# A third Winograd level in five more pairs of a tuned f32 matrix product, and two early sums moved into another round

## The chip, the cores and the metric

The kernel runs on one core of one Trainium2 chip, as one launch. The metric is the device time of that core in microseconds, the median of several runs. The engines are called PE (TensorE, matrix products), DVE (VectorE), ACT (ScalarE), POOL (GpSimd) and SP (SyncE, which here only issues transfers).

## The reference, cut to what matters

Everything is float32. `x` has 32 samples of 128 channels by 2048.

```python
# first half: mix the channels, then a 2048 x 2048 layer with a low-rank update
att = softmax(mlp(cond_128))                       # 32 x 8
agg_w = einsum('bk,koi->boi', att, weight)         # one 128 x 128 kernel per sample
h = einsum('boi,bih->boh', agg_w, x) + agg_b
out = einsum('bsd,od->bso', h, W) + bias           # 4096 x 2048 by 2048 x 2048
upd = einsum('ebsr,eor,e->bso', einsum('bsd,erd->ebsr', h, A), Bf, coeffs * scales)
x = x + out + upd
# second half: grouped convolution, then a small two-layer network on each of 16 heads of permuted columns
c = conv1d(x, conv_weight, groups=4, pad=4) + ctx + bias
t = c[:, perm] as heads of 128
x = x + (gelu(t @ up[h]) @ down[h])[unperm]
```

The low-rank update is folded into the weight: the kernel first makes W' = W plus the sum of the scaled products of A and Bf, and then multiplies the 4096 rows of x by W'. The channel mix acts on the channels of a sample and the layer on the columns, so the mix is applied after the product.

## The kernel before, in words

**The big product.** x W' is made by Winograd's form of Strassen's method: 7 products of half-size blocks stand in the place of 8. The outer level gives seven rounds, in the order `ROUNDS = ("P1", "P2", "P6", "P7", "P5", "P3", "P4")`. Each round works through 8 groups g (512 rows of x each). Inside a round `multiply` (L341) makes a group's 512x1024 by 1024x1024 block with 7 products of the second level; each product is 4 matmuls of 128x128 by 128x512, and the profile counts two passes of PE for every f32 matmul. Results go to a PSUM bank and from there are added by DVE (or copied first by ACT) into accumulators of 128x2048.

**The third level.** In some pairs of groups (g even and g + 1, the table `PAIRS`) two of the seven products, P2 and P4, are not made for each group alone: `multiply_third` (L536) makes them for both groups together with seven products of quarter blocks ("quarters", matmuls of 256 columns, L607). Their weights come from `third_weights` (`P_q`), their inputs from `third_inputs` (`sq`). In the pairs of `MORE` a second family, P3 and P7, is made in that way too (`multiply_more`, L482, quarters at L514, weights `P_v` from `more_weights`, inputs `sv` from `more_inputs`). A group is then left with 5 or 3 products of its own, and a pair has 7 or 14 quarters.

**Between the products.** After each product the function calls `between(j)`, in which the main loop gives other engines something to do: `mixed_kernel` (DVE, 8 chained operations on 128x128 for one k range of a sample's mixing kernel, `ags`), weights' differences for the third level, row sums of W', and the loads of later steps.

**Buffers and queues.** Nearly all tiles of 128x2048 (x, weights, their combinations, accumulators) come from one pool of `SLOTS = 26` buffers through `slot`. The pool gives a new tile the buffer of a tile that was released earlier, and the first write to it waits for the last reader. Every engine works through its instructions in program order, which is written out by hand. SP issues loads of x (`x_load`), of weights and of partial results (`part_load`) and the stores of accumulators. POOL makes `x_combine` (four operations of 128x512, `s_P`), inner weights (16), outer weights and `outer_sums`, and issues some stores itself.

**Early sums.** Rounds P6 and P5 multiply sums of blocks of x, which `outer_sums(g, ts)` makes: eight operations on POOL, and a store of each result (`s1` for P5, `s2` for P6 and P3). For the first `EARLY = 2` groups this is done ahead of P6, and the three x tiles are loaded for it alone:

```python
k_early = g if r == "P2" else -1
if 0 <= k_early < EARLY:
    early_x = [x_load(k_early, *k) for k in ((1, 0), (1, 1), (0, 0))]
def between(j):
    if j == 3 and 0 <= k_early < EARLY:
        outer_sums(k_early, early_x)
```

**The rest.** P1 starts while W' is still being made, block by block (`w_make_two`, stored to DRAM as `wb_d`). Beside the last round and after it come the convolution, the mix (L842, L853) and the per-head networks (L986, L997), which the change does not touch.

Of the kernel before, what the change touches and what calls it, by code (L numbers as in the profile page):

```python
# [17 lines left out]
B = 32  # L18
L = 2048
QW = 512  # L20
KEXP = 8
# [27 lines left out]


PAIRS = {
    "P1": (1, 2, 3), "P2": (0, 1, 2, 3), "P6": (0, 1, 2, 3), "P7": (0, 1, 2, 3),
    "P5": (0, 1, 2, 3), "P3": (0, 1, 2, 3), "P4": (0,),
}
MORE = {"P7": (1, 2), "P3": (1, 2)}
ENDS = ("P1", "P4")
EARLY = 2

# [2 lines left out]
def adaln_ffn_kernel(  # L61
# [355 lines left out]
    def in_pair(r, g):  # L417
        return g // 2 in PAIRS[r]

    rest = []  # L420

    def third_inputs(i, eng):

        (x11, x12), (x21, x22) = (
            [xa[n][:, 1, :, h * NQ : (h + 1) * NQ] for h in range(2)] for n in (i, i + 1)
        )
        tt = eng.tensor_tensor
        t = slot(f"sq_{i}", (P, 4, 2, NQ))
        tt(t[:, 0], x21, x22, ALU.add)
        tt(t[:, 1], t[:, 0], x11, ALU.subtract)  # L430
        rest.append((t[:, 2], x11, x21))
        rest.append((t[:, 3], x12, t[:, 1]))
        if eng is nc.gpsimd:
            sums_rest(eng)
        return {
            "P1": x11, "P2": x12, "P3": t[:, 3], "P4": x22,
            "P5": t[:, 0], "P6": t[:, 1], "P7": t[:, 2],
        }

    def sums_rest(eng):  # L440
        while rest:
            eng.tensor_tensor(*rest.pop(0), ALU.subtract)

    def more_weights(name, rhs):

# [36 lines left out]
    def multiply_more(r, g, lhs, rhs, accs, between, families):  # L482

        px, py = bank(), bank()
        if g % 2 == 0:
            both = [accs]
            held.extend((both, {}, {}))
        both, *sums = held
        if g % 2:
            both.append(accs)  # L490

        def add(ps, *to):
            for si, oi in to:
                for acc in accs:
                    nc.vector.tensor_tensor(acc[:, si, oi], ps, acc[:, si, oi], ALU.add)  # L495

        def product(k, ps, first, last):
            for kc in range(4):
                nc.tensor.matmul(  # L499
                    ps, lhsT=lhs[k][:, bass.ts(kc, P)], rhs=rhs[k][kc],  # L500
                    start=first and kc == 0, stop=last and kc == 3, skip_group_check=True,
                )

        def quarter(n, k):

            quarters, x = families[n]
            qs = sums[n]
            if k in ("P1", "P5", "P2"):
                qs[k] = bank()
            ps = qs[{"P6": "P1", "P7": "P1", "P4": "P1", "P3": "P5"}.get(k, k)]  # L510
            first, last = k in ("P1", "P2", "P5"), k in ("P2", "P3", "P4")
            for i, out in enumerate(halves(ps)):
                for kc in range(2):
                    nc.tensor.matmul(  # L514
                        out, lhsT=x[k][:, 1 - i if n else i, bass.ts(kc, P)],
                        rhs=quarters[i][k][kc],
                        start=first and i == 0 and kc == 0, stop=last and i == 1 and kc == 1,
                        skip_group_check=True,
                    )
            b, h = {  # L520
                "P1": (0, 0), "P2": (0, 0), "P6": (0, 1), "P5": (1, 1), "P7": (1, 1),
                "P3": (0, 1), "P4": (1, 0),
            }[k]
            cols = slice(h * NQ, (h + 1) * NQ)
            for acc in both[b]:
                part = acc[:, :, n, cols]
                nc.vector.tensor_tensor(  # L527
                    part, ps.rearrange("p (s n) -> p s n", s=2), part, ALU.add
                )
                if n:  # L530
                    part = acc[:, 1, 0, cols]
                    nc.vector.tensor_tensor(part, ps[:, NQ : 2 * NQ], part, ALU.add)
            if last:
                done(ps)

        def quarters_of(*nks):  # L536
            if g % 2:
                for n, k in nks:
                    quarter(n, k)

        product("P1", px, True, False)
        add(px, (0, 0))
        between(0)
        quarters_of((0, "P6"), (0, "P5"))
        product("P5", py, True, True)
        add(py, (1, 1), (0, 1))
        done(py)
        between(1)
        quarters_of((1, "P6"), (0, "P7"))
        product("P6", px, False, True)  # L550
        add(px, (0, 1), (1, 1), (1, 0))
        done(px)
        between(2)
        if g % 2 == 0:
            quarter(0, "P1")
            quarter(0, "P2")
            between(3)
            quarter(1, "P1")
            between(4)
            quarter(1, "P2")  # L560
            between(5)
            return
        quarters_of((1, "P5"), (0, "P3"))
        between(3)
        quarters_of((1, "P7"), (0, "P4"))
        between(4)
        quarters_of((1, "P3"))
        between(5)
        quarters_of((1, "P4"))
        held.clear()  # L570
        for b, accs in enumerate(both):
            for (_, new), acc in zip(ADDED[r], accs):
                part_store(new, g - 1 + b, acc, nc.sync)
# [648 lines left out]
    for i, (r, g) in enumerate(steps):  # L1222
        ri = i // NG
        last_round = ri + 1 == len(ROUNDS)
        if i + 1 < len(steps):
            if i + 1 not in xs:
                xs[i + 1] = x_loads(*steps[i + 1])
            if not last_round:
                lhs[i + 1] = x_combine(*steps[i + 1], xs.pop(i + 1))
                if g == 2 * PAIRS[r][0]:  # L1230
                    quarters, quarter_ops = third_weights(r, rhs)
                if in_pair(r, g) and g % 2 == 0 and g > 0 and r != "P6":
                    sq = third_inputs(i, nc.gpsimd)
                    if in_more(r, g):
                        sv = more_inputs(i)
                if r in MORE and g == 2 * MORE[r][0] - 1:
                    more, more_ops = more_weights(r, rhs)
        if i == 0:
# [41 lines left out]
        if last_round:  # L1280
            stage(k0, stage_first)

        k_early = g if r == "P2" else -1
        if 0 <= k_early < EARLY:
            early_x = [x_load(k_early, *k) for k in ((1, 0), (1, 1), (0, 0))]

        def between(j):

            if j == 3 and 0 <= k_early < EARLY:
                outer_sums(k_early, early_x)  # L1290

            b = (ri - 1) * (NG - 2) + g + 1 if ri > 0 else g - (NG - 2)
            if (g in range(1, NG - 1) if ri > 0 else g >= NG - 2) and b < B:
                k = j - 2 if r == "P5" and g == 1 else j
                if 0 <= k < KEXP // 2:
                    mixed_kernel(b, (2 * k, 2 * k + 1))
            if ri == 0 and j == 2:
                for k in blocks[6 + 2 * g : 8 + 2 * g]:
                    wt[k] = w_load(*k)
            if j < 4 and quarter_ops:  # L1300
                nc.vector.tensor_tensor(*quarter_ops.pop(0), ALU.subtract)
            if j < 4 and more_ops:
                nc.vector.tensor_tensor(*more_ops.pop(0), ALU.subtract)
            if i == NG - 1 and j == 3:
                olds_load(i + 1)
            if j == 3 and ahead and steps[i + 2][0] == "P6":
                xs[i + 2] = x_loads(*steps[i + 2])
            if ri == 0 and j in (1, 3) and unsummed:
                row_sums(*unsummed.pop())
            if ri == 0 and j == 5 and unsummed_first:  # L1310
                t = unsummed_first.pop(0)
                tt = nc.vector.tensor_tensor
                tt(wsum[:, 0, 0], wsum[:, 0, 0], t[:, 0, 0], ALU.add)
                tt(wsum[:, 0], wsum[:, 0], t[:, 1], ALU.add)
            if last_round:
                if j == 1 and i + 1 < len(steps):
                    lhs[i + 1] = x_combine(*steps[i + 1], xs.pop(i + 1))
                    olds_load(i + 1)
                if j == 4 and i + 2 < len(steps):
                    xs[i + 2] = x_loads(*steps[i + 2])  # L1320
                if j in (2, 4):
                    stage(k0 + j // 2, stage_first)
                if j % 2:
                    stage_third(k0 + j // 2)
                else:
                    stage(k0 + j // 2, stage_second)
# [10 lines left out]
            multiply(r, g, lhs.pop(i), rhs, olds.pop(i), between)  # L1337
        xa.pop(i - 1, None)
        ss.pop(i - 1, None)
        if in_pair(r, g) and g % 2 == 0 and (g == 0 or r == "P6" or last_round):  # L1340
            sq = third_inputs(i, nc.gpsimd if r in ENDS else nc.vector)
        next(chain, None)
        if i > 4:
# [95 lines left out]
```

## Time and profile before

| | |
|---|---|
| median of 3 runs | 2577.21 us (2575.98 to 2579.15) |
| profiled execution | 2577.27 us, span 2575.5 us, granted clock 0.999 |
| largest group of PE | L986 and L997, 460 us each (the last third of the span) |
| DVE, largest group | L714, `ags`, 195.5 us in 224 records |
| POOL, largest group | L735, 174.5 us |
| P1 starts / P2 / P6 (first matmul on PE) | 45.9 us / 296.4 / 482.8 |
| P7 / P5 / P3 / P4 | 669.4 / 853.1 / 1038.8 / 1222.6 |

The profiled execution lies within 0.1 us of the median, so its rows stand for the median run. A row of a timeline gives the start, the duration, the engine, the line, the operation with its tiles, the shape and the number of records; in brackets stands the idle time of the engine before it and what ended it. Buffer and group numbers are left out of names there.

### The profile page before, as it was taken

To read this page: it belongs to the slowest core of one execution; us is meant where nothing else is said; L and a number is where in the kernel's file an instruction comes from. 1 tells how busy PE (TensorE), PEld (TensorE's weight loads), DVE (VectorE), ACT (ScalarE), POOL (GpSimd) and SP (SyncE) were. 2 spreads that over 40 slices of the span, in tenths; PEclk is the share of its full clock that TensorE was granted. 3 is DMA by queue.
4 is the path that set the end of the run, shared out by engine and by line. 5 is a ranking of instruction groups with operands and counts; after the bars stand their busy time and mean duration, and the time that the engine had idled before them with its cause. 6 is when DMAs were issued, how large, how long until landed. Compare 5 with 4: busy or idle time off the path is not lost.

```text
span 2575.5 us, 22121 instructions
## 1 busy us (share of the span) xinstructions
PE 2564.0 (100%) x7142; PEld 1355.4 (53%) x7142; DVE 1579.5 (61%) x2450; ACT 532.3 (21%) x1099; POOL 1394.2 (54%) x1158
## 2 busy tenths in 40 slices
PE   9999999999999999999999999999999999999999
PEld 4455555555566555566554554455555554455543
DVE  5665576666585576675476666666666666667611
ACT  0000000000000000000011244444444444444432
POOL 7431788878997736989432134444344434434222
PEclk9999999999999999999999999999999999999999
DMA  7452588579366486574866887787777877777432
GB/s 322 182 211 113 198 338 344 212 285 370 151 249 263 196 337 273 221 287 168 281 230 210 279 290 266 224 259 230 226 223 234 252 246 223 222 251 237 164 123 90
DMA packets 186867, 610.42 MB, mean 237 GB/s; under 512 B 17664, under 2 KB 91904, under 8 KB 142336
## 3 DMA queue, kind: packets, MB, share of 16 engines
q1 hardware_dynamic: 147936, 473.48, 51.2%
q0 software_dynamic: 32992, 132.14, 15.2%
q10 hardware_dynamic: 5824, 3.40, 0.5%
q8 instruction: 57, 0.93, 0.1%
q14 instruction: 58, 0.48, 0.1%
HBM read 372.45 MB, written 202.94 MB: 223 GB/s over the span
## 4 chain that ended last, share of the span: by engine, by line
PE 95%; DVE 3%; DMA 2%; issue 0%; SPq 0%; POOLq 0%; ACT 0%; ACTq 0%; DVEq 0%
PE bank L594 26%; PE bank L986 17%; PE bank L997 17%; PE bank L607 9%; PE bank L357 7%; PE bank L842 6%; PE bank L750 4%; PE bank L499 3%; PE bank L223 3%; PE bank L514 2%; DMA w<-in_WT 1%; DVE ags L714 1%; DMA xt<-in_xT 0%; DVE u L527 0%; DVE u L495 0%
## 5 line engine op out<-in xcount | busy, mean ns | idle before, releaser
L986 PE MATMUL bank<-t,ws 128*128 128x512 f32 x1024 | 460.3, 592 | 0.0
L997 PE MATMUL bank<-gl,ws 128*128 128x512 f32 x1024 | 460.1, 592 | 0.0
L1004 POOL DMA_INDIRECT out<-t,orow x128 | 152.3, 1189 | 535.8 <-DVE t L1002 452.5
L989 ACT ACTIVATE gl<-bank 128x512 f32<-128x512 f32 x512 | 306.1, 598 | 433.3 <-PE bank L986 414.1
L997 PEld LDWEIGHTS bank<-gl,ws 128*128 128x128 f32 x1024 | 194.6, 190 | 232.9 <-issue 231.5
L986 PEld LDWEIGHTS bank<-t,ws 128*128 128x128 f32 x1024 | 194.6, 190 | 226.6 <-issue 222.2
L594 PE MATMUL bank<-P_t,s_P 128*128 128x512 f32 x640 | 284.3, 592 | 0.4 <-ACT m_P L589 0.4
L1002 DVE TENSOR_TENSOR t<-bank,t 128x512 f32<-128x512 f32 x128 | 88.4, 690 | 320.2 <-PE bank L997 309.4
L735 POOL TENSOR_TENSOR x<-x,fb 128x512 f32<-128x512 f32 x128 | 174.5, 1392 | 198.9 <-DMA x<-in_x 136.4
L741 ACT ACTIVATE bank<-w,aggb 128x512 f32<-128x512 f32 x128 | 80.8, 684 | 880.3 <-DMA w<-w_d 867.8
L283 POOL TENSOR_TENSOR xt<-xt,xt 128x512 f32<-128x512 f32 x120 | 159.0, 1358 | 104.6 <-DMA xt<-in_xT 88.4
L714 DVE SCALAR_TENSOR_TENSOR ags<-mix,att_bc,ags 128x128 f32<-128x128 f32 x224 | 195.5, 873 | 4.7
L594 PEld LDWEIGHTS bank<-P_t,s_P 128*128 128x128 f32 x640 | 121.4, 190 | 140.4 <-issue 136.6
L587 DVE TENSOR_TENSOR u<-bank,u 128x512 f32<-128x512 f32 x156 | 101.6, 686 | 147.4 <-PE bank L594 135.1
L594 PE MATMUL bank<-wo_P,s_P 128*128 128x512 f32 x416 | 184.7, 592 | 0.0
L319 POOL TENSOR_TENSOR s_P<-xt 128x512 f32<-128x512 f32 x52 | 68.8, 1323 | 204.0 <-DMA xt<-in_xT 164.2
L970 POOL DMA_INDIRECT t<-hx_d,row x128 | 131.1, 1025 | 56.6 <-issue 25.6
L587 DVE TENSOR_TENSOR p<-bank,p 128x512 f32<-128x512 f32 x96 | 64.6, 687 | 117.8 <-PE bank L594 117.1
L594 PEld LDWEIGHTS bank<-wo_P,s_P 128*128 128x128 f32 x416 | 79.0, 190 | 89.2 <-issue 87.3
L842 PE MATMUL bank<-va,tw_l 128*128 128x256 f32 x512 | 121.5, 380 | 0.7 <-DVE va L826 0.7
L853 ACT ACTIVATE cv<-bank,ctxb 128x128 f32<-128x128 f32 x256 | 73.0, 368 | 234.6 <-PE bank L842 234.6
L753 DVE TENSOR_TENSOR x<-bank,x 128x512 f32<-128x512 f32 x128 | 88.1, 690 | 50.8 <-POOL x L735 21.9
(242 smaller groups left out, 3869.0 us busy)
## 6 DMA issues: line engine op xcount, KB each, us to landing
xt<-in_xT SPq DMA_DIRECT2D x84, 1024.0 KB
u<-u_d SPq DMA_DIRECT2D x40, 1024.0 KB
wo_P<-wb_d SPq DMA_DIRECT2D x36, 1024.0 KB
u<-c_d SPq DMA_DIRECT2D x64, 512.0 KB
x<-in_x SPq DMA_DIRECT2D x32, 1024.0 KB
xg<-x SPq DMA_DIRECT2D x256, 128.0 KB
hx_d<-x1t SPq DMA_DIRECT2D x32, 1024.0 KB
hx_d<-ht SPq DMA_DIRECT2D x32, 1024.0 KB
```

The lines of the kernel that those rows point to most:

```text
L283: nc.gpsimd.tensor_tensor(out[:, i, j], a[:, i, j], b[:, i, j], op)
L357: nc.tensor.matmul(ps, lhsT=lhs[k][:, bass.ts(kc, P)], rhs=rhs[k][kc], start=first and kc == 0, stop=last and kc == 3, skip_group_check=True,)
L587: nc.vector.tensor_tensor(to, ps, to, ALU.add)
L594: nc.tensor.matmul(ps, lhsT=lhs[k][:, bass.ts(kc, P)], rhs=rhs[k][kc], start=first and kc == 0, stop=last and kc == 3, skip_group_check=True,)
L607: nc.tensor.matmul(out, lhsT=sq[k][:, i, bass.ts(kc, P)], rhs=quarters[i][k][kc], start=first and i == 0 and kc == 0, stop=last and i == 1 ...
L714: nc.vector.scalar_tensor_tensor(ag, mix[:, k], att, ag, ALU.mult, ALU.add)
L735: nc.gpsimd.tensor_tensor(xt[:, f], xt[:, f], late["fb"][:, f], ALU.add)
L842: nc.tensor.matmul(out, lhsT=w[:, 2 * i + r], rhs=rhs, start=first and r == 0, stop=last and r == 1, skip_group_check=True,)
L986: nc.tensor.matmul(pu, lhsT=w[:, m * P : (m + 1) * P], rhs=t[:, 0], start=True, stop=True)
L989: nc.scalar.activation(gl[m], pu, AF.Gelu)
L997: nc.tensor.matmul(pd, lhsT=w[:, (MC + m) * P : (MC + m + 1) * P], rhs=gl[m], start=(m == 0), stop=(m == MC - 1),)
L1004: nc.gpsimd.indirect_dma_start(out=out, out_offset=bass.IndirectOffsetOnAxis(ap=orow[:, g, h : h + 1], axis=0), in_=t[:, 1], in_offset=None,)
```

## The change

Five pairs get one level more: P1's pair 0, until now made by `multiply`, is made by `multiply_third`; pair 1 of P2, pair 1 of P6, pair 3 of P7 and pair 3 of P3 get the second family. The inputs of the third level are made in parts (`sums_rest(eng, n)`), so that some of the operations can follow later. In the rounds of `MORE` the 48 calls of `mixed_kernel` are handed out from a list, one after each of the first four products in groups 2 and 4 and two in the other groups from 1 on, where until now the groups 1 to 6 had eight each. `k_early` becomes `g - 6` in P1: the first sums, with their six loads of x and their stores, are issued in P1's groups 6 and 7 and no longer in P2's groups 0 and 1. Row sums of W' are given other places in P1.

```diff
--- before.py
+++ after.py
@@ -49,10 +49,10 @@
 
 
 PAIRS = {
-    "P1": (1, 2, 3), "P2": (0, 1, 2, 3), "P6": (0, 1, 2, 3), "P7": (0, 1, 2, 3),
+    "P1": (0, 1, 2, 3), "P2": (0, 1, 2, 3), "P6": (0, 1, 2, 3), "P7": (0, 1, 2, 3),
     "P5": (0, 1, 2, 3), "P3": (0, 1, 2, 3), "P4": (0,),
 }
-MORE = {"P7": (1, 2), "P3": (1, 2)}
+MORE = {"P6": (1,), "P7": (1, 2, 3), "P3": (1, 2, 3), "P2": (1,)}
 ENDS = ("P1", "P4")
 EARLY = 2
 
@@ -419,17 +419,19 @@
 
     rest = []
 
-    def third_inputs(i, eng):
+    def third_inputs(i, eng, later=False):
 
         (x11, x12), (x21, x22) = (
             [xa[n][:, 1, :, h * NQ : (h + 1) * NQ] for h in range(2)] for n in (i, i + 1)
         )
         tt = eng.tensor_tensor
         t = slot(f"sq_{i}", (P, 4, 2, NQ))
-        tt(t[:, 0], x21, x22, ALU.add)
-        tt(t[:, 1], t[:, 0], x11, ALU.subtract)
-        rest.append((t[:, 2], x11, x21))
-        rest.append((t[:, 3], x12, t[:, 1]))
+        rest.append((t[:, 0], x21, x22, ALU.add))
+        rest.append((t[:, 1], t[:, 0], x11, ALU.subtract))
+        if not later:
+            sums_rest(eng, 2)
+        rest.append((t[:, 2], x11, x21, ALU.subtract))
+        rest.append((t[:, 3], x12, t[:, 1], ALU.subtract))
         if eng is nc.gpsimd:
             sums_rest(eng)
         return {
@@ -437,9 +439,9 @@
             "P5": t[:, 0], "P6": t[:, 1], "P7": t[:, 2],
         }
 
-    def sums_rest(eng):
-        while rest:
-            eng.tensor_tensor(*rest.pop(0), ALU.subtract)
+    def sums_rest(eng, n=4):
+        for _ in range(min(n, len(rest))):
+            eng.tensor_tensor(*rest.pop(0))
 
     def more_weights(name, rhs):
 
@@ -542,6 +544,8 @@
         add(px, (0, 0))
         between(0)
         quarters_of((0, "P6"), (0, "P5"))
+        if g % 2:
+            sums_rest(nc.vector)
         product("P5", py, True, True)
         add(py, (1, 1), (0, 1))
         done(py)
@@ -1222,6 +1226,10 @@
     for i, (r, g) in enumerate(steps):
         ri = i // NG
         last_round = ri + 1 == len(ROUNDS)
+        if g == 0:
+            b = (ri - 1) * (NG - 2) + 2
+            mixes = [(b + n // KEXP, n % KEXP) for n in range((NG - 2) * KEXP)]
+            mixes = [m for m in mixes if m[0] < B]
         if i + 1 < len(steps):
             if i + 1 not in xs:
                 xs[i + 1] = x_loads(*steps[i + 1])
@@ -1229,10 +1237,13 @@
                 lhs[i + 1] = x_combine(*steps[i + 1], xs.pop(i + 1))
                 if g == 2 * PAIRS[r][0]:
                     quarters, quarter_ops = third_weights(r, rhs)
-                if in_pair(r, g) and g % 2 == 0 and g > 0 and r != "P6":
-                    sq = third_inputs(i, nc.gpsimd)
-                    if in_more(r, g):
-                        sv = more_inputs(i)
+                if in_pair(r, g) and g % 2 == 0 and g > 0:
+                    if r != "P6":
+                        sq = third_inputs(i, nc.gpsimd)
+                    elif in_more(r, g):
+                        sq = third_inputs(i, nc.vector, True)
+                if in_more(r, g) and g % 2 == 0:
+                    sv = more_inputs(i)
                 if r in MORE and g == 2 * MORE[r][0] - 1:
                     more, more_ops = more_weights(r, rhs)
         if i == 0:
@@ -1280,7 +1291,7 @@
         if last_round:
             stage(k0, stage_first)
 
-        k_early = g if r == "P2" else -1
+        k_early = g - 6 if r == "P1" else -1
         if 0 <= k_early < EARLY:
             early_x = [x_load(k_early, *k) for k in ((1, 0), (1, 1), (0, 0))]
 
@@ -1290,14 +1301,19 @@
                 outer_sums(k_early, early_x)
 
             b = (ri - 1) * (NG - 2) + g + 1 if ri > 0 else g - (NG - 2)
-            if (g in range(1, NG - 1) if ri > 0 else g >= NG - 2) and b < B:
+            if (g in range(1, NG - 1) if ri > 0 else g >= NG - 2) and b < B and r not in MORE:
                 k = j - 2 if r == "P5" and g == 1 else j
                 if 0 <= k < KEXP // 2:
                     mixed_kernel(b, (2 * k, 2 * k + 1))
+            if r in MORE and 0 < g and j < 4:
+                for _ in range(1 if g in (2, 4) else 2):
+                    if mixes:
+                        b, k = mixes.pop(0)
+                        mixed_kernel(b, (k,))
             if ri == 0 and j == 2:
                 for k in blocks[6 + 2 * g : 8 + 2 * g]:
                     wt[k] = w_load(*k)
-            if j < 4 and quarter_ops:
+            if i and j < 4 and quarter_ops:
                 nc.vector.tensor_tensor(*quarter_ops.pop(0), ALU.subtract)
             if j < 4 and more_ops:
                 nc.vector.tensor_tensor(*more_ops.pop(0), ALU.subtract)
@@ -1305,9 +1321,9 @@
                 olds_load(i + 1)
             if j == 3 and ahead and steps[i + 2][0] == "P6":
                 xs[i + 2] = x_loads(*steps[i + 2])
-            if ri == 0 and j in (1, 3) and unsummed:
+            if ri == 0 and unsummed and (j in (1, 3) and (i, j) != (1, 3) or (i, j) == (3, 2)):
                 row_sums(*unsummed.pop())
-            if ri == 0 and j == 5 and unsummed_first:
+            if (i, j) in ((2, 5), (3, 0), (3, 4), (4, 0)) and unsummed_first:
                 t = unsummed_first.pop(0)
                 tt = nc.vector.tensor_tensor
                 tt(wsum[:, 0, 0], wsum[:, 0, 0], t[:, 0, 0], ALU.add)
@@ -1337,7 +1353,9 @@
             multiply(r, g, lhs.pop(i), rhs, olds.pop(i), between)
         xa.pop(i - 1, None)
         ss.pop(i - 1, None)
-        if in_pair(r, g) and g % 2 == 0 and (g == 0 or r == "P6" or last_round):
+        if in_more(r, g) and r == "P6":
+            sums_rest(nc.vector, 2)
+        elif in_pair(r, g) and g % 2 == 0 and (g == 0 or r == "P6" or last_round):
             sq = third_inputs(i, nc.gpsimd if r in ENDS else nc.vector)
         next(chain, None)
         if i > 4:
```

Lines after L440 are four further down in the changed kernel.

## The prediction

> **What bounds the kernel now.** I read the totals of the page first, then the chain that ended last, then the timelines of PE, POOL and SP around the end of round P1, because that is where the moved sums go.
>
> ```profile
> PE 2564.0 (100%) x7142; PEld 1355.4 (53%) x7142; DVE 1579.5 (61%) x2450; ACT 532.3 (21%) x1099; POOL 1394.2 (54%) x1158
> ...
> PE 95%; DVE 3%; DMA 2%; issue 0%; SPq 0%; POOLq 0%; ACT 0%; ACTq 0%; DVEq 0%
> ```
>
> TensorE works 2564.0 of 2575.5 us. All other engines have idle time, so only two things count: how many passes PE makes, and any new hole in PE. A hole costs its full length. The difference between two kernels that this kernel's measurement can tell from no change is about 0.2%, here 5 us.
>
> PE at the end of P1 (start, duration, operation, number of passes):
>
> ```profile
> 247.61 1.89 PE L607 MATMUL bank<-P_q,xt 128*128 128x256 f32 x8
> 249.34 3.60 PE L594 MATMUL bank<-w,xt 128*128 128x512 f32 x8
> ...
> 267.18 3.60 PE L594 MATMUL bank<-w,xt 128*128 128x512 f32 x8
> 270.62 7.03 PE L594 MATMUL bank<-P_t,s_P 128*128 128x512 f32 x16
> 277.48 7.03 PE L594 MATMUL bank<-w,s_P 128*128 128x512 f32 x16
> ...
> 287.80 5.34 PE L607 MATMUL bank<-P_q,sq 128*128 128x256 f32 x24
> 292.98 1.03 PE L607 MATMUL bank<-w,sq 128*128 128x256 f32 x4
> ...
> 296.44 3.60 PE L594 MATMUL bank<-w,xt 128*128 128x512 f32 x8
> ```
>
> Two prices come from it. A pass of 512 columns takes (284.35 - 277.48)/16 = 0.429 us (284.35 is where the next row starts), a pass of 256 columns (292.98 - 287.80)/24 = 0.216 us. Call E the end of the quarters of group 5, 249.34. Group 7 starts at 267.18, makes P1 (3.43 us) and P5 (3.43 us), and starts its product P6 at 274.05, E + 24.7. From there 10.3 us of group 7 and 12.1 us of quarters remain; P2 starts at 296.44.
>
> POOL over the same time and a little after:
>
> ```profile
> 258.62 1.26 POOL L319 TENSOR_TENSOR s_P<-xt 128x512 f32<-128x512 f32 x1 [36.81 <-DMA xt<-in_xT]
> ...
> 268.70 1.26 POOL L252 TENSOR_TENSOR P_t<-w 128x512 f32<-128x512 f32 x1
> ...
> 289.45 1.27 POOL L319 TENSOR_TENSOR s_P<-xt 128x512 f32<-128x512 f32 x1
> ...
> 327.52 4.93 POOL L283 TENSOR_TENSOR xt<-xt,xt 128x512 f32<-128x512 f32 x4
> 332.75 0.56 POOL L277 DMA_DIRECT2D s_d<-xt  x1 [0.30 <-POOL xt L283]
> ```
>
> The reader sees that POOL cannot begin the end of P1 before x of group 7 lands: it starts 9.3 us after E, and then has 28 operations (combinations of group 7, its third-level inputs, P2's inner weights) until 289.45, 30.8 us. Today the next thing is s_P of P2's group 0. The first sums come only in P2.
>
> **Part 1, third level in five more pairs.** A pair that goes one level deeper, P1's pair 0 from second to third or the others from one family of quarters to two, loses 32 passes of 512 and gains 56 of 256: 56 x 0.216 - 32 x 0.429 = -1.65 us. The five together: -8.25 us, all on PE. Beside it DVE gets 44 evictions of 256 columns and 35 of 2x256, less 2 of 512 (0.41 and 0.69 us each by the timeline of P7's pair 1: 41 us over the whole), and POOL 20 operations of 512 (1.27 to 1.39 us) and 16 of 256 (0.72 to 1.18): 37 to 47 us. I take both as hidden by the 996 and 1181 us in which those engines stand still. Where they are dense the cover can fail: the first pair with two families in P7 and P3 shows stalls of 0.75, 0.64, 0.34 and 1.02 us, 1.4 us a pair, so P2's and P6's new pair could add 0 to 2.8 us. P7's and P3's pair 3 look like P7's pair 2, where PE is busy 45.00 of 45.00 us between 762 and 807, so nothing there. At P1's start POOL now makes third_weights and pair 0's inputs ahead of the weight stores, and later weight loads wait for the buffers of those stores: 0 to 4 us by my walk, 0.5 taken.
>
> **Part 2, mixes spread out.** The same 48 per round, 0.87 us each on average, but 4 fewer in group 2 of P7 and P3, just before those four stalls. They sum to 2.75 us; the gain is 0 to 2.75. I take 1.9, and with the 0.5 above that is -1.4.
>
> **Part 3, the first sums (outer_sums 0 and 1) go from P2's to P1's end.** The removal in P2 gains nothing, PE has no hole over 0.5 us there. The cost is in the addition, and it is one of buffers. The instruction order of the changed kernel with its waits shows that the six extra x tiles take the last free ones of the 26 buffers. The chain, with E' for the end of group 5's quarters in the changed kernel:
> - POOL comes to the sums of group 0 only behind the 28 operations, at E' + 9.3 + 30.8 = 40.1. The eight pieces and two stores cost 4.93 + 0.86 + 4.93 + 0.86 (0.86 is the 0.30 wait and 0.56 issue of the store row): the pieces end at 50.8, the store of s2 is issued by 51.7. In before the second such group took 12.4 us between 343.86 and 356.25, so up to 1.7 more.
> - The load of x for P2's group 0 takes the buffer of xt_000, so it waits for the last piece, 50.8. A 1 MB load landed 7.9 us after its issue at 250.72 in before, with another transfer beside it, and in 5.5 us when alone (issued at 139.86, POOL's start at 145.33). s_P20, 5.0 us, sits on POOL between the two sums and ends at about 63.
> - The load of xt_111, needed by the sums of group 1, takes the buffer of xt_011 and waits until the store of s2 has landed; loads behind it on SP wait too. The stores of these sums landed in 5.5 us at best, 10.6 in the median, 11.9 at worst: 57 to 64, taken as 62 since three more 1 MB transfers run at that time. Then 5.5 to 7.9 us of load: 62.7 to 72, taken as 68.5.
> - The sums of group 1 take 4.93 + 0.86 + 4.93 = 10.7 us: end at 73.4 to 82.7 (up to 1.7 more), taken as 79.
> - ACT's first copy into group 7's accumulator (L593, m_P) has been given the buffer of xt_100, which the last of these pieces reads. The copy, 0.6 us, therefore waits for it. PE's product P6 of group 7 goes into the PSUM bank that this copy empties, so PE stops after P5, at E' + 24.7.
>
> PE resumes at about 79.6 and should have been there at 24.7: a hole of 55 us (74.0 to 85 gives 49.3 to 60). Taken: 54.5, as x may land a little earlier. Behind the waiting copy on ACT are group 7's other copies and the issue of a small store; behind the waiting loads on SP are p1 of P2's group 0 (which takes xt_110's buffer) and the stores of P1's last pair. Nothing of that is late a second time: after the hole PE has 22.4 us of P1 left, and P2's inputs land in those.
>
> One more cost follows from such a hole. The first six passes of the program, 4 of 512 and 2 of 256 columns, would take 2.15 us by the prices above and took 4.36 (1.47 to the next row at 5.83), though the column of the granted clock shows 1.00 there. After a hole of this length I expect the same again, 0 to 2.2 us; taken 2.0.
>
> The Trainium skill ("TensorE: Matmul & The Clock Gate", section "What's actually happening") says that the array drops to half its clock after an idle window of some 3.4 us and needs as long a busy one to come back. An estimate by that page is 3.4 / 2 = 1.7 us for this hole, and the sum would be 0.3 us lower; it speaks against this change, as the holes of before were too short for it.
>
> The Trainium skill ("DMA: Bandwidth & Descriptors", section "Anatomy of one DMA") fits a transfer by 2.0 us plus its bytes over 436 GB/s, which would be 4.4 us for 1 MB by estimate. The landings in this trace are longer, 5.5 at the least; with 4.4 for each the chain would end near 72 and the hole be 47 us, the sum 7.5 us lower; the measured ones decide.
>
> **The sum.** The profiled execution took 2577.27 us (span 2575.5 and 1.8 around it), beside a median of 2577.21, so no conversion is needed. 2577.27 - 8.25 - 1.4 + 54.5 + 2.0 = 2624.1, given as 2624.
>
> **The rivals.**
> - No hole, the other side (faster). If the buffers that the sums give back come in time, only PE's saving is left: 2577.27 - 8.25 - 1.4 = 2567.6, between 2566 and 2571. It decides whether the last piece of the second sums ends before E' + 24.7. For it: POOL is idle for 36.81 us before 258.62, so there is room for 22 us of sums before E. Against it: in POOL's order they stand behind the combination of group 7 and the inner weights, and the first cannot start before x lands. 9%.
> - The hole is only at P2's start. If group 7's copies find a buffer, P2 still needs x and the accumulator p1 of its group 0, and p1's load takes xt_110's buffer, so it waits for the store of s1 and the last piece, 79, and lands in 5.5. P2 would start at E' + 47.1; PE can fill three banks (3 x 3.43 us) before it must wait for one that DVE adds into p1. The hole is then 79 + 5.5 - 47.1 - 10.3 = 27 us: 2577.27 - 8.25 - 1.4 + 27 + 2 = 2596.6. For it: SP's order has that wait as well. Against it: ACT's copy comes first. 5%.
> - DVE or POOL becomes the bound in the deeper pairs on top of the hole: at 1.4 us in each of five pairs, 7 us, 2631. For it: the four stalls in P7 and P3 are DVE's. Against it: pair 2 of P7 without any. 14%, inside the range.
>
> **How the numbers follow.** 72% for the forecast, 14% for it with late engines, 5% for the hole at P2's start alone, 9% for none. The range: the short end of the chain is a hole of 49.3, no slow restart and all of 2.75 gained, 2577.27 - 8.25 + 49.3 - 2.75 = 2615.6; x of group 7 landing in 5.5 in place of 7.9 us takes 2.4 more off, and POOL's 48 operations at the best pitch of the rows (1.22 for 1.26 us) about 2: 2611. The long end is 60 + 2.2 + 2.8 + 4 = 69 us, 2638. 2611 to 2638 leaves out the two rivals with a smaller hole, 14%, and some tail. Faster by over 0.2% is the first rival, 0.09; within 0.2%, 0.01, since no case ends there; slower 0.90.
>
> **What would show it.** PE's timeline of the changed kernel would have one hole of 49 to 60 us after P5 of P1's group 7, released by ACT's copy into m_P, and POOL's timeline the sums of group 1 ending just before. P2 would begin some 52 us later than 296.44, and from there every stage would run at its old length less 1.65 us in each deepened pair. Wrong would be: no hole over 5 us in P1, the sums of both groups ending before group 7's P6, or holes of several us in P2's, P6's, P7's or P3's deeper pairs.

## The result, and the profile after

The changed kernel takes 2624.23 us (median of 6 runs, 2622.44 to 2625.56), beside 2576.60 for the kernel before in the same runs: a ratio of 1.0181, with a 95% interval of 1.0171 to 1.0191. It is 1.8% slower. The profiled execution took 2622.44 us, 45.2 more than the one of before.

The totals of the page after, its row of granted clocks over 40 slices of the span, and the shares of the engines in the chain that ended last:

```profile
PE 2556.7 (98%) x7262; PEld 1378.4 (53%) x7262; DVE 1616.8 (62%) x2527; ACT 533.3 (20%) x1099; POOL 1434.7 (55%) x1194
...
PEclk9999599999999999999999999999999999999999
...
PE 94%; POOL 2%; DMA 2%; DVE 1%; issue 0%; POOLq 0%; SPq 0%; ACT 0%; ACTq 0%; DVEq 0%
```

PE is busy 7.3 us less than before and the span is 45.1 us longer. POOL, which had no share of the chain of before, now has 2% of it, and one slice of the clock, the fifth, is at half: a hole of the kind that the kernel before did not have. PE's timeline shows it:

```profile
247.03 3.60 PE L598 MATMUL bank<-w,xt 128*128 128x512 f32 x8
...
264.89 3.60 PE L598 MATMUL bank<-w,xt 128*128 128x512 f32 x8
268.33 3.60 PE L598 MATMUL bank<-P_t,s_P 128*128 128x512 f32 x8
325.16 5.48 PE L598 MATMUL bank<-P_t,s_P 128*128 128x512 f32 x8 [53.23 <-ACT m_P L593]
330.47 7.03 PE L598 MATMUL bank<-w,s_P 128*128 128x512 f32 x16
```

E', the end of group 5's quarters, is 247.03. PE stops after P5 of P1's group 7 at 271.8, E' + 24.7, and waits 53.2 us for ACT's copy into m_P. POOL's timeline over that stretch carries the chain:

```profile
287.01 4.92 POOL L283 TENSOR_TENSOR xt<-xt,xt 128x512 f32<-128x512 f32 x4
292.23 0.56 POOL L277 DMA_DIRECT2D s_d<-xt  x1 [0.30 <-POOL xt L283]
292.81 4.92 POOL L283 TENSOR_TENSOR xt<-xt,xt 128x512 f32<-128x512 f32 x4
298.02 0.56 POOL L277 DMA_DIRECT2D s_d<-xt  x1 [0.30 <-POOL xt L283]
303.72 1.25 POOL L319 TENSOR_TENSOR s_P<-xt 128x512 f32<-128x512 f32 x1 [5.14 <-DMA xt<-in_xT]
...
313.77 4.92 POOL L283 TENSOR_TENSOR xt<-xt,xt 128x512 f32<-128x512 f32 x4 [5.01 <-DMA xt<-in_xT]
...
319.57 4.92 POOL L283 TENSOR_TENSOR xt<-xt,xt 128x512 f32<-128x512 f32 x4
```

The chain that ended last has the two transfers between the sums, the store of s2 and the load of xt_111 (start and length):

```profile
298.02 10.78 DMA s_d<-xt
308.82 4.79 DMA xt<-in_xT
```

The first sums end at 297.7, the store of s2 is issued at 298.02, SP issues xt_111 at 308.8, the second sums start at 313.77 and end at 324.5, and ACT copies at once (the timeline of ACT):

```profile
324.52 1.08 ACT L593 COPY m_P<-bank 128x512 f32<-128x512 f32 x2 [58.11 <-POOL xt L283]
```

This row names the last reader of the buffer, a piece of sums that has nothing to do with group 7's product.

### The profile page after: what moved, and what is told of

Its sections match the earlier page's. It is cut to its first block, busy times and chain, and to the rows that moved or that the text cites. A ratio compares the mean times of both kernels' runs of the same rounds, so it can differ in the third digit from the quotient of the medians.

```text
span 2620.6 us, 22480 instructions
## 1 busy us (share of the span) xinstructions
PE 2556.7 (98%) x7262; PEld 1378.4 (53%) x7262; DVE 1616.8 (62%) x2527; ACT 533.3 (20%) x1099; POOL 1434.7 (55%) x1194
## 4 chain that ended last, share of the span: by engine, by line
PE 94%; POOL 2%; DMA 2%; DVE 1%; issue 0%; POOLq 0%; SPq 0%; ACT 0%; ACTq 0%; DVEq 0%
PE bank L598 21%; PE bank L990 17%; PE bank L1001 17%; PE bank L611 8%; PE bank L516 7%; PE bank L846 6%; PE bank L501 6%; PE bank L357 5%; PE bank L754 4%; PE bank L223 2%; PE bank L180 1%; DMA xt<-in_xT 1%; POOL xt L283 1%; DMA s_d<-xt 0%; POOL sq L444 0%; DVE ags L718 0%
## 5 line engine op out<-in xcount | busy, mean ns | idle before, releaser
L598 PE MATMUL bank<-P_t,s_P 128*128 128x512 f32 x544 | 243.4, 596 | 53.7 <-ACT m_P L593 53.7
L319 POOL TENSOR_TENSOR s_P<-xt 128x512 f32<-128x512 f32 x52 | 68.5, 1318 | 236.7 <-DMA xt<-in_xT 156.6
L598 PEld LDWEIGHTS bank<-P_t,s_P 128*128 128x128 f32 x544 | 103.9, 191 | 175.3 <-issue 117.6
L591 DVE TENSOR_TENSOR u<-bank,u 128x512 f32<-128x512 f32 x132 | 85.4, 686 | 102.2 <-PE bank L598 99.2
L598 PE MATMUL bank<-wo_P,s_P 128*128 128x512 f32 x320 | 142.1, 592 | 0.0
L846 PEld LDWEIGHTS bank<-va,tw_l 128*128 128x128 f32 x512 | 97.0, 190 | 41.9 <-issue 31.2
L754 PE MATMUL bank<-u,agl 128*128 128x512 f32 x256 | 115.1, 592 | 0.0
```

What stands on the lines that cost most here:

```text
L598: nc.tensor.matmul(ps, lhsT=lhs[k][:, bass.ts(kc, P)], rhs=rhs[k][kc], start=first and kc == 0, stop=last and kc == 3, skip_group_check=True,)
L754: nc.tensor.matmul(pm, lhsT=ag, rhs=u[:, f], start=False, stop=True, skip_group_check=True)
L846: nc.tensor.matmul(out, lhsT=w[:, 2 * i + r], rhs=rhs, start=first and r == 0, stop=last and r == 1, skip_group_check=True,)
```

## The experiments

**1. Only the early sums moved.** The kernel before with one line changed:

```diff
-        k_early = g if r == "P2" else -1
+        k_early = g - 6 if r == "P1" else -1
```

> The kernel before with nothing but k_early moved to P1's groups 6 and 7. Theory: the same chain of waits, since the buffers stand the same: a hole of 52 to 55 us before product P6 of group 7 and 1.9 us of slow restart, so 2576.6 + 55.3 = 2632 us, 2629 to 2635. Rival (part of the hole comes from the extra work of P1's third-level pair 0): hole under 45 us, time under 2625.

Measured: 2632.30 us, ratio 1.0212 (1.0195 to 1.0229). Its PE timeline has one row with a long wait in P1:

```profile
331.25 5.82 PE L594 MATMUL bank<-P_t,s_P 128*128 128x512 f32 x8 [53.31 <-ACT m_P L589]
```

The hole is as long as in the changed kernel, so the third level in pair 0 has no part in it.

**2. Group 7's accumulator gets its buffer first.**

```diff
+        if r == "P1" and g == NG - 1:
+            kept[i] = slot(f"m_{r}{g}", (P, 2, 2, QW))
+            nc.vector.memset(kept[i][:, 0, 0, 0:1], 0.0)
         k_early = g - 6 if r == "P1" else -1
...
-        accs = ... [slot(f"m_{r}{g}", ...)]
+        accs = ... [kept.pop(g) if g in kept and r == "P1" else slot(...)]
```

> The changed kernel, with the accumulator of P1's group 7 given its buffer before the x tiles of the second early sum (it is written once, in one column, by DVE). POOL and its order stay as they are. Theory (a buffer, not POOL's pace, stops PE at group 7): no hole at group 7. P2 then starts at E' + 47.1 but its x lands at about 56.7 (its buffer comes with the last piece of the first sums), and p1 of group 0, now behind the x tiles of the second sums on SP, lands at 72 to 75, so PE waits once more for about 10 us: holes of 20 us in all, 2 to 3 us of slow restart, 2624.2 - 55.3 + 22.5 = 2591 us, 2586 to 2597. Rival (POOL is too late with its own work, whatever the buffers): the holes sum to over 45 us, time over 2614.

Measured: 2593.93 us, ratio 1.0063 (1.0046 to 1.0080). On POOL the sums run as late as before the edit (second sums from 317.16 to 327.9), but PE goes through group 7. Its rows with a wait are now in P2's groups 0 and 1:

```profile
307.12 6.67 PE L598 MATMUL bank<-w,xt 128*128 128x512 f32 x8 [10.51 <-DMA xt<-in_xT]
324.23 6.63 PE L598 MATMUL bank<-P_t,s_P 128*128 128x512 f32 x8 [7.00 <-DVE p L591]
338.51 3.70 PE L598 MATMUL bank<-w,xt 128*128 128x512 f32 x8 [0.78 <-DMA xt<-in_xT]
```

The first waits for x of P2's group 0, the second for DVE's addition into p1. The two blocks of 8 passes last 6.6 us each in place of 3.6, so the slow passes cost about 3 us after each of the two holes, 6 in all, where 2 to 3 were expected. The holes are 18.3 us in all and not 20, which makes up for a part of it. One buffer for one tile moves 30 us: the hole of group 7 is a want of a buffer and not of POOL's time.

**3. One early sum in place of two.**

```diff
-EARLY = 2
+EARLY = 1
```

> The changed kernel with EARLY = 1: only the sums of group 0 are made in P1's end; those of group 1 are made in P6 as for groups 2 to 7. Theory: three buffers fewer are taken, group 7's accumulator gets a free one, no hole at group 7. P2's x still lands at E' + 56.7 (hole of 9.6 us), and p1 of group 0 waits for the store of the first s2, landing at about 67, another 4 us: holes of 14 us, 2 to 3 us of slow restart, 2624.2 - 55.3 + 16.5 = 2585 us, 2581 to 2590. Rival (POOL's load): one sum of 10.7 us and one store of 0.9 us less shortens the hole by about 12 us: 2612.

Measured: 2590.83 us, ratio 1.0052 (1.0036 to 1.0069), 5.8 above the theory, just outside its range, and 21 below the rival. PE waits 10.3 us for x at P2's start, near the 9.6 expected, then only 1.0 for p1, where I had 4. What I had left out is in P5:

```profile
306.19 5.46 PE L598 MATMUL bank<-w,xt 128*128 128x512 f32 x8 [10.29 <-DMA xt<-in_xT]
316.10 3.67 PE L598 MATMUL bank<-P_t,s_P 128*128 128x512 f32 x8 [1.02 <-DVE p L591]
...
876.41 4.07 PE L598 MATMUL bank<-wo_P,s_P 128*128 128x512 f32 x5 [3.61 <-DVE u L591]
```

With the slow passes behind it, this wait costs 5.5 us by the starts of the passes, about what the theory missed. With EARLY = 1, P5's group 1 loads two tiles of x instead of one finished sum; that this causes the wait was not tested.

**4. P2's inner weights behind the first sums on POOL.**

```diff
-        if g == NG - (1 if ri else 2) and ri < len(ROUNDS) - 1:
+        if g == NG - 1 and ri and ri < len(ROUNDS) - 1:
             nxt = inner_weights(ROUNDS[ri + 1], ...)
...
                 outer_sums(k_early, early_x)
+            if ri == 0 and g == NG - 2 and j == 3:
+                nxt.update(inner_weights(ROUNDS[1], ...))
```

> The changed kernel with one thing in another order on POOL: P2's inner weights (16 operations, 20.7 us) are made behind the sums of group 0 and no longer ahead of them. Theory (the hole is the chain POOL, store, load, POOL, copy): the sums of group 0 end at E' + 30, the store lands at 41, xt_111 at 46 beside POOL's inner weights (until 51.5) and s_P20 (56.5), the sums of group 1 run from there to 67.3, so PE resumes at 68 and not at 78.1: hole 43 us, 10 us less, 2614 us, 2611 to 2618. Rival (the hole's length is set by transfers that the other order does not touch): time within 3 us of 2624.

Measured: 2614.84 us, ratio 1.0143 (1.0127 to 1.0158). The starts of the first pieces of both sums in POOL's timeline, and the row after the hole in PE's:

```profile
269.06 4.98 POOL L283 TENSOR_TENSOR xt<-xt,xt 128x512 f32<-128x512 f32 x4
...
306.20 4.92 POOL L283 TENSOR_TENSOR xt<-xt,xt 128x512 f32<-128x512 f32 x4
```

```profile
317.58 5.36 PE L598 MATMUL bank<-P_t,s_P 128*128 128x512 f32 x8 [43.03 <-ACT m_P L593]
```

The hole is 10.2 us shorter, as the walk along the chain said: of 20.7 us taken out ahead of the first sums, half returns because POOL now makes the inner weights between the two sums.

**5. PE kept busy through the hole.** 60 matmuls into a bank that nobody reads:

```diff
         product("P5", py, True, False)
         add(1, 1, py)
         between(1)
         turn(1, early)
+        if r == "P1" and g == NG - 1:
+            pw = bank()
+            for _ in range(60):
+                nc.tensor.matmul(pw, lhsT=lhs["P1"][:, bass.ts(0, P)], rhs=rhs["P1"][0],
+                                 start=True, stop=True, skip_group_check=True)
+            done(pw)
```

> The changed kernel with 60 idle matmuls of 512 columns (120 passes, 51.5 us) on PE between P5 and P6 of P1's group 7, into a bank that nobody reads: PE is busy through nearly all of the hole, and the chain that ends it stays. Theory (the slow passes after the hole come from PE having been idle): PE is free again at E' + 76.2, waits about 2 us for the copy, and the passes of P6 take 0.429 us from the first on: 1.9 us less, 2622.3 us, and the first P6 block of 8 passes 3.4 us long in place of 5.3. Rival (the passes are slow for another reason, such as the transfers that run at that time): the block stays at 5.3 us and the time at 2624.

Measured: 2622.97 us, ratio 1.0176 (1.0160 to 1.0193); the time alone cannot tell this from 1.0181 (in the profiled execution a wait for weights near 138 us is 1.5 us longer than in the changed kernel's, nearly as much as the slow passes cost). PE's timeline can:

```profile
273.48 51.66 PE L650 MATMUL bank<-w,xt 128*128 128x512 f32 x120
327.04 3.70 PE L598 MATMUL bank<-P_t,s_P 128*128 128x512 f32 x8 [1.90 <-ACT m_P L593]
```

The eight passes of P6 last 3.70 us and no longer 5.48. In the changed kernel the table by stretches gives the clock beside the passes (columns: stretch, its length, busy time and instructions of PE, PEld, DVE, ACT, POOL, granted clock, DMA share, GB/s):

```profile
300.00:325.10 25.10, 0.00 (x0) 0.00 (x0) 0.00 (x0) 0.58 (x2) 15.67 (x14) 0.50 0.63 240
325.10:328.60 3.50, 3.44 (x4) 1.52 (x5) 0.00 (x0) 0.49 (x2) 0.24 (x1) 0.50 0.83 206
328.60:340.00 11.40, 11.40 (x34) 6.17 (x33) 2.69 (x5) 1.17 (x2) 0.00 (x0) 0.99 0.37 128
```

The clock stays at 0.50 for 3.5 us after PE resumes. Four passes run at half rate, and the hole costs 1.86 us beyond its length (0.59 + 3 x 0.42). The stretch after the wait in the profile of this run, with as much transferred beside it (DMA share 0.84 and 0.83), has the full clock, so the rival's transfers are not the cause:

```profile
327.00:330.60 3.60, 3.56 (x9) 1.65 (x10) 0.00 (x0) 0.48 (x1) 0.23 (x1) 1.00 0.84 212
```

**6. The whole change, with the early sums put back into P2.**

```diff
-        k_early = g - 6 if r == "P1" else -1
+        k_early = g if r == "P2" else -1
```

> The changed kernel with k_early put back to P2's groups 0 and 1; everything else of the change stays. Theory (the hole at group 7 of P1 is the first sums' doing alone): the hole of 53.4 us and the slow restart of 1.9 us go, 2624.2 - 55.3 = 2569 us, 2566 to 2571, thus 6 to 10 us faster than before. Rival (the deeper pairs and the new places of other work make part of the loss): a hole of over 5 us stays in P1 or in a deeper pair, and the time lies above 2577.

Measured: 2604.49 us, ratio 1.0106 (1.0089 to 1.0123). The theory "the move alone costs, the rest pays" fell: the hole of P1 is gone, and another stands in P2's pair 0. From the timelines of PE and DVE:

```profile
356.54 6.46 PE L611 MATMUL bank<-P_q,sq 128*128 128x256 f32 x16 [32.85 <-DVE p L619]
```

```profile
355.37 0.42 DVE L1319 TENSOR_TENSOR P_v<-w 128x256 f32<-128x256 f32 x1 [35.59 <-POOL xt L283]
355.71 1.48 DVE L619 TENSOR_TENSOR p<-bank,p 128x512 f32<-128x512 f32 x2
```

It is the same kind of wait in another place. DVE's first write into the second family's weight tile (P_v) has been given the buffer of an early x tile and waits for the last piece of the second sums; DVE's evictions stand in order behind it, and PE behind those. So in P2 the new family and the early sums do not fit together, and in P1's end the early sums and group 7 do not.

**7. Early sums in P2, no second family there.** The edit of 6, and

```diff
-MORE = {"P6": (1,), "P7": (1, 2, 3), "P3": (1, 2, 3), "P2": (1,)}
+MORE = {"P6": (1,), "P7": (1, 2, 3), "P3": (1, 2, 3), "P2": ()}
```

> The changed kernel with the first sums back in P2's groups 0 and 1 and without the second family in P2's pair 1; the four other deeper pairs and the mixes stay. Theory (in P2 the second family's two weight tiles and the sums' six x tiles want the same buffers; either of them alone fits): no hole over 2.5 us anywhere, 2577.4 - 4 x 1.65 - 1.4 = 2569 us, 2566 to 2573. Rival (the sums collide in P2 with something else of the change): a hole of over 10 us stays in P2's pair 0, over 2580.

Measured: 2572.34 us (median of 11) beside 2577.70, ratio 0.9980 (0.9971 to 0.9989). PE's busy share is whole again:

```profile
PE 2557.0 (100%) x7238; PEld 1372.9 (53%) x7238; DVE 1617.1 (63%) x2505; ACT 532.6 (21%) x1099; POOL 1423.0 (55%) x1182
```

This version is faster than both kernels, by 5.4 us (0.2%) against before. Expected were the four pairs' 6.6 us and 1.4 from the other changes, 8.0: the pairs' 6.6 lies within the interval (2.8 to 7.5 us), the 8.0 does not.

**8. The second family in P2's pair 2.** As 7, but with `"P2": (2,)`.

> As the run before (first sums in P2's groups 0 and 1), but with the second family in P2's pair 2 in place of pair 1: its weights are made from group 3 on, when the sums' x tiles are gone. Theory: no hole in pair 0, and 1.65 us less than without it, 2567.5 us, 2564 to 2572. Rival (the same want of buffers, one pair later: loads of P6's outer weights now wait for matmuls of pair 2 and land too late for P6's inner weights): a hole of over 5 us at P2's end or P6's start, over 2574.

Measured: 2577.87 us, ratio 0.9999 (0.9990 to 1.0009). Pair 0 has no hole, but pair 1 has one of 5.4 us, again through P_v. From the timeline of DVE:

```profile
374.17 0.42 DVE L1319 TENSOR_TENSOR P_v<-w 128x256 f32<-128x256 f32 x1 [8.17 <-DMA tw_d<-tw]
```

This time the buffer comes from a tile of the convolution's weights, whose store lands 10.6 us after its issue at 363.46. The passes behind this hole run at half rate for 5.2 us and cost 2.6 us more, so a hole of 5.4 us takes 8.0. Neither theory nor rival had that place; the rival's kind of cause was right.

**9. The mixes at their old places.** As 7, with the list of mixes taken out and eight in each of the groups 1 to 6 again.

> The first kernel of this group (first sums in P2, no second family there) with the mixes where they stood before the change: eight in each of the groups 1 to 6. Theory (the mixes of group 2 make DVE late in the pairs 1 with two families): the stalls of 0.75, 0.64, 0.34 and 1.02 us of before come back, in P6's pair 1 up to 1.4 more: 1 to 4 us slower than the first of this group. Rival: the mixes' place does not matter, within 0.5 us, and the stalls that are left have another cause.

Measured: 2572.56 us, ratio 0.9979 (0.9970 to 0.9988), 0.2 us from run 7. PE's gaps in the pairs with two families are 0.42, 0.64, 0.25 and 0.86 us here and 0.39, 0.79, 0.20 and 0.90 in run 7. They stand at the ends of P6's pair 1, P7's pair 2 and P3's pairs 1 and 2; the two stalls of P7's pair 1, which the kernel before has, do not come back. The theory fell: where the mixes stand does not set these stalls. What does was not settled.

## Why the prediction was right

2624 was forecast and 2624.23 measured. The mechanism was the forecast one; that the totals agree to 0.2 us is luck. The profiled execution, which the terms below are read from, is the fastest of the six (2622.44), and as measured the terms add up to that, some 1.7 us less than forecast: the hole was 1.1 shorter than taken, the restart 0.1, and the rest gained 0.4 more. The terms, each beside what the profiled execution shows:

- **PE's passes**, -8.25: the trace has 160 passes of 512 columns less and 280 of 256 more. At the pitches of the timelines (0.4294 and 0.2158 with a digit more) that is -8.27, the -8.25 of the prediction; the three digits that the prediction shows would give -1.63 a pair and not its -1.65.
- **The chain to the hole.** From E': first sums end at 50.8 forecast, 50.7 measured; s_P20 ends at 63, measured 61.7; the store of s2 landed at 62, measured 61.8; xt_111 at 68.5, measured 66.7; second sums end at 79, measured 77.5; PE resumes at 79.6, measured 78.1. The hole: 54.5 forecast, 53.4 in the passes' starts. The load of xt_111 took 5.0 us and not 6.5; part of that had been taken off already. The taken landing of the store was a choice between 57 and 64, so that it came out to 0.2 us is chance; the path is not. The operations of POOL ahead of 289.45 are 24 (4 + 4 + 16) and not the 28 of the prediction; its 30.8 us were read from the rows and hold. P2 begins at 349.43, 53.0 us later than before, where some 52 were expected.
- **The slow restart**, 2.0: 1.86, and run 5 shows that PE's idleness is its cause. The size was partly luck: behind the holes of the other runs it was 1.8 to 3.1 us, in runs 2, 6 and 8 clearly more than the 2.2 taken as its most. The estimate by the Trainium skill ("TensorE: Matmul & The Clock Gate", section "What's actually happening") was 1.7, and the half clock for 3.5 us that the table shows agrees with what that page says; the 6.0 us at half clock after each hole of run 2 are more than this estimate has.
- **The transfers.** The Trainium skill ("DMA: Bandwidth & Descriptors", section "Anatomy of one DMA") has its fit for transfers that GpSimd issues, and 4.4 us for 1 MB is the estimate by it. Two stores of run 4 that had no other large transfer beside them landed after 4.2 us each, which agrees. On the chain of the changed kernel the store of s2 had two 1 MB loads beside it and landed after 10.8. The load of xt_111, which SP issues and that fit does not cover, took 5.0. The rows of before, most of them with other transfers beside them, were the better guide to this chain.
- **The rest**, -1.4: all of PE's other gaps together shrank by 1.8 us (45.15 + 8.27 - 53.4 - 1.86). But the step behind it was wrong: I gave 1.9 of it to the mixes, and run 9 finds nothing there. In the pairs with two families the four largest gaps went from 2.3 to 1.9 us; the remainder is small gaps before and in P1, in P2 and in the tail that happened to close. One reading was wrong as well: the largest of the four stalls of before, 1.02 us, is not in a first pair with two families but at the end of P3's pair 2 (PE is busy 45.24 of 46 us between 1130 and 1176), so P7's quiet pair 2 did not speak for all second pairs. That P7's and P3's pair 3 have no gap over 0.2 us came true all the same. The weight load that was feared cost 0.2 us more than before (PE's wait at 138.19), and 1.5 to 1.9 more in four of the experiments.

The rivals: "no hole" did not occur, and run 6 shows that its price, 2567.6, was not to be had by leaving the early sums where they were either; I had named neither that P2's own new family wants buffers nor that the move makes room for it. "The hole only at P2's start" was priced at 27 us, 2596.6; run 2 makes that case, with 2593.93: 18.3 us of holes and 6 of slow passes, where the price had 27 and 2. "Late engines in the deeper pairs" was not seen: P2's pair 1 and P6's pair 1 have no gap over 0.2 us in the changed kernel.

## What to carry to other kernels

When a step is moved in a kernel whose tiles share one pool of buffers, follow each new tile to the tile whose buffer it takes and to that tile's last reader: the wait shows up at an engine that has nothing to do with the moved step. The price is then the length of the chain of transfers and slow engines from the release back to its start, and here it came out to 1 us from single rows of the profile before. Undo the parts of a change in pairs too: two parts can each be harmless and want the same buffers together.

## What the runs showed of the hardware

After a hole of 53 us the granted clock stood at 0.50 for another 3.5 us of work; after the holes of 10 and 7 us of run 2 it did so for 6.0 us each, after the 5.4 us of run 8 for 5.2. The loss was 1.9, 3.0, 3.0 and 2.6 us, so here it did not grow with the hole. In the traces' record of the clock the stretches at 0.50 inside the program last 54.61 us (changed kernel), 13.65 and 10.24 (run 2) and 6.83 (run 8), which is 16, 4, 3 and 2 steps of 3.41 us. That fits a clock that is set anew only every 3.41 us, so that the loss depends on where between two steps PE resumes; no run moved a hole to test this. With idle matmuls in the hole the clock stayed at 1.00.

At the start of the program the same slow passes stand under a granted clock that the column shows as 1.00; the record behind the column has its first entry at 5.7 us in the kernel before and at 4.5 in the changed one, and the passes are slow up to about there.

A 1 MB store that POOL issued landed after 10.8 us when two 1 MB loads ran beside it (the store of s2), and after 4.2 us when no large transfer did (two stores of run 4).
